# Keys and queries of a head as seven block products, context keys read from memory, turned probabilities evicted by ScalarE

## The chip, the cores and the metric

The kernel runs on one core of a Trainium2 chip. The metric is the device time of one launch in microseconds (us), from the first to the last instruction and what lies around it. The core has five engines that work side by side, each through its own instructions in order: TensorE (PE) multiplies matrices and transposes, VectorE (DVE) and ScalarE (ACT) work element by element and read TensorE's results out of the banks of PSUM, GpSimd (POOL) does the same more slowly, and SyncE (SP) issues transfers between memory and the on-chip buffers.

## What is computed

The reference is one decoder layer on `x` (16 sequences of 256 tokens, width 256) and a context `ctx_1024` (16 × 77 rows, width 256), everything in fp32: three sublayers, each `x = layernorm(x + f(x))`. Cut to what matters:

```python
x = _layernorm(x + _L0_attn_ref(x, ...))              # a small recurrence over time
x = _layernorm(x + _L0_xattn_ref(ctx_1024, x, ...))   # attention, below
x = _layernorm(x + _L0_ffn_ref(x, ...))               # 8 experts, top 2, capacity

# the attention: x = context rows, latents = tokens; H = 8 heads of DH = 128
xn = _layernorm(x, gamma_media, beta_media)
ln = _layernorm(latents, gamma_lat, beta_lat)
q = ln @ Wq + bq
kv_input = jnp.concatenate([xn, ln], axis=1)          # 77 + 256 = 333 rows
k, v = jnp.split(kv_input @ Wkv + bkv, 2, axis=-1)
sim = jnp.einsum('bhid,bhjd->bhij', q * DH ** (-0.5), k)
attn = jax.nn.softmax(sim, axis=-1)
out = jnp.einsum('bhij,bhjd->bhid', attn, v)          # heads are put side by side
return out @ Wo + bo
```

So each of the 16 sequences (called batches below) has 8 heads, and each head has queries for 256 tokens and keys for 333 rows, of which 256 come from the same normalised tokens as the queries and 77 from the context.

## The kernel before

The work goes in three stages. A first stage loads weights, runs the recurrence of batch 0, normalises half of the context rows (five of ten tiles of 128 rows), computes their values for all heads and stores them to memory (`vc_d`), and prepares batch 0. The middle stage walks through all 128 heads (16 batches × 8) in one written-out software pipeline. The last stage runs the experts.

In the middle stage, iteration i does the following in program order. `head_kq(i)`: keys (L587, 333 columns) and queries (L592, 256 columns) of head i, each a sum of two products over the two halves of the width; ScalarE evicts both with the bias (L589, L594). Then the steps that a table lays on this head, such as the recurrence of later batches (`rec_in`, `rec_state`), `prep_keys` (turns the normalised tokens into `kvt`, 333 columns with the context rows copied in by GpSimd, L507), `prep_sums` and `prep_values` (values of the next batch by seven block products, L552), `project_pairs` (the attention's output projection, seven block products of 128×128, L729), `turn_tokens`, `score_experts`, `choose` and `dispatch` (expert choice), and `settle` (stores the batch's tokens, L786). Then `head_out(i−2)`: probabilities times values (L639), evicted by ScalarE (L647). Then `head_softmax(i)`: scores (L602) into one two-bank PSUM tile of which there is only one, the row maximum (DVE, L604), two exponentials with their sums (ScalarE, L608), reciprocal (L610) and normalising (DVE, L613). Then `head_turn(i−1)`: six transposes of the normalised probabilities (L625); DVE evicts four of them (bank pa, L627) and ScalarE two (bank po, L628). The late steps of the table follow.

In the table, batch 0 also computes the values of the other five tiles of context rows (`context`, L470), and each batch prepares its successor. The recurrence of four batches is finished at once (`rec_state`, with a small scan at its end that begins with the product L385). Within these limits a scheduler of the framework chooses the issue order on each engine; where the code says `issue_after`, an instruction is held behind another. SP issues all loads and stores of these stages in one order, among them the values of a batch's context rows (L549), the token stores (L786) and, early on, 34 clears of the expert buffer.

A seven-product scheme forms a 2×2 block matrix product with seven block products instead of eight, from sums and differences of the blocks. The kernel before uses it for the values and for the output projection, the sums of weights being made once.

## Time and profile before

| | |
|---|---|
| median of 3 runs | 1165.93 us (1164.4 to 1166.26) |
| profiled execution | 1174.61 us |
| its span, first to last instruction | 1172.9 us |
| first scores of head (0,0) start | 51.4 us |
| heads | 51.4 to about 1022 us |
| TensorE busy | 1140.7 us (97%), 5436 instructions |
| VectorE busy | 812.1 us (69%) |
| ScalarE busy | 494.5 us (42%) |
| GpSimd busy | 321.2 us (27%) |
| mean granted TensorE clock | 0.998 |

A line of the profile names the source line, the engine, the operation, the tile written and the tiles read, and the shapes. A count follows an x. In timelines the first two numbers are start and duration in microseconds; what stands in brackets is the idle time of the engine before the instruction and who ended it. In groups, total busy time and the mean of one (ns) are followed by the engine's idle time ahead of the group. Where instructions of TensorE overlap, the step from start to start is the price of one, and the duration is longer. Weight loads (PEld) run beside the products.

### The profile page before, as it was taken

The numbers are of one execution on the slowest core, as the hardware profiler recorded it, in microseconds if no ns is written. First come the engines' busy times: TensorE is split into PE (matmuls) and PEld (weight loads), VectorE is DVE, ScalarE is ACT, GpSimd is POOL, SyncE is SP. The second block draws the span as 40 slices with busy tenths as digits, with TensorE's granted clock in tenths as the row PEclk, the third lists the DMA queues.
The fourth block names the chain that finished last, engine by engine and source line by source line (L and its number), as shares of the span: only waits on it lengthen the run. The fifth ranks groups of instructions, "written<-read, shape, count | busy, mean of one in ns | idle before, by whom it ended". The sixth has DMA issues, their size and how long they took to land. (4 is left out here: it accounts for less than half of the span.)

```text
span 1172.9 us, 16419 instructions
## 1 busy us (share of the span) xinstructions
PE 1140.7 (97%) x5436; PEld 833.5 (71%) x5436; DVE 812.1 (69%) x2367; ACT 494.5 (42%) x1298; POOL 321.2 (27%) x564
## 2 busy tenths in 40 slices
PE   7999999999999999999999999999999999999996
PEld 3465676777787877677777777687877778876664
DVE  6655878686757776876678767766576664665665
ACT  3344444443444444444445444444444443523331
POOL 2211243113311331232213322232122212144454
PEclk9999999999999999999999999999999999999999
DMA  7740101001000010000000100000001000045752
GB/s 253 217 144 33 35 22 37 12 28 39 24 25 17 28 37 22 27 29 19 15 10 24 37 14 10 14 19 14 10 14 46 24 10 12 21 162 137 180 161 87
DMA packets 47149, 60.67 MB, mean 52 GB/s; under 512 B 7941, under 2 KB 37102, under 8 KB 47064
## 3 DMA queue, kind: packets, MB, share of 16 engines
q1 hardware_dynamic: 39686, 50.31, 13.5%
q0 software_dynamic: 6048, 9.22, 3.1%
q8 instruction: 43, 0.70, 0.3%
q14 instruction: 42, 0.34, 0.1%
q10 hardware_dynamic: 1330, 0.10, 0.1%
HBM read 36.33 MB, written 30.78 MB: 57 GB/s over the span
## 5 line engine op out<-in xcount | busy, mean ns | idle before, releaser
L639 PE MATMUL po<-ptt,v 128*128 128x256 f32 (+1 forms) x768 | 190.9, 382 | 1.6 <-DVE rs L610 1.6
L639 PEld LDWEIGHTS po<-ptt,v 128*128 128x128 f32 (+1 forms) x768 | 141.5, 190 | 53.1 <-issue 35.5
L587 PE MATMUL pk<-kvt,wkv_s 128*128 128x333 f32 x512 | 165.3, 444 | 0.0
L602 PE MATMUL s<-kt,qt 128*128 128x333 f32 x512 | 164.3, 442 | 0.0
L604 DVE TENSOR_REDUCE nm<-s 128x2 f32<-128x666 f32 x128 | 108.3, 846 | 54.3 <-PE s L602 54.1
L608 ACT ACTIVATE p<-s,nm 128x333 f32<-128x333 f32 x256 | 135.4, 535 | 22.6 <-DVE nm L604 21.9
L647 ACT ACTIVATE ot<-po,bkv_s 128x256 f32<-128x256 f32 x128 | 60.8, 475 | 172.0 <-PE po L639 171.0
L592 PE MATMUL pq<-kvt,wq_s 128*128 128x256 f32 x512 | 131.2, 379 | 0.0
L587 PEld LDWEIGHTS pk<-kvt,wkv_s 128*128 128x128 f32 x512 | 91.1, 191 | 45.9 <-issue 23.2
L602 PEld LDWEIGHTS s<-kt,qt 128*128 128x128 f32 x512 | 96.5, 189 | 30.9 <-issue 0.5
L592 PEld LDWEIGHTS pq<-kvt,wq_s 128*128 128x128 f32 x512 | 96.7, 189 | 30.5 <-issue 0.5
L628 ACT COPY ptt<-pb 77x256 f32<-77x256 f32 x128 | 47.2, 369 | 163.1 <-PE pb L625 163.1
L613 DVE TENSOR_SCALAR pn<-p,rs 128x333 f32<-128x333 f32 x256 | 100.8, 429 | 3.3
L921 POOL DMA_INDIRECT xg<-xs,sidx x64 | 65.6, 1025 | 89.2 <-DVE sidx L918 58.5
L627 DVE COPY ptt<-pa 128x512 f32<-128x512 f32 x128 | 87.2, 682 | 0.6 <-PE pa L625 0.6
L625 PEld LDWEIGHTS pa<-ident,pn 128*128 128x128 f32 x512 | 63.9, 141 | 29.3
L589 ACT ACTIVATE kt<-pk,bkv_s 128x333 f32<-128x333 f32 x128 | 68.9, 538 | 24.6 <-PE pk L587 23.8
L625 PE MATMUL pa<-ident,pn 128*128 128x128 f32 x512 | 76.8, 273 | 0.0
L339 DVE SCALAR_TENSOR_TENSOR cv<-hp,cw,cv 128x512 f32<-128x512 f32 (+1 forms) x108 | 73.9, 691 | 1.4
L594 ACT ACTIVATE qt<-pq,bqs 128x256 f32<-128x256 f32 x128 | 61.0, 477 | 18.8 <-PE pq L592 14.9
L324 PE MATMUL ph<-xT,inw 128*128 128x512 f32 (+1 forms) x144 | 63.4, 570 | 5.0 <-DMA inw<-in_in_wT 4.9
L1183 PE MATMUL pf<-w,it 128*128 128x256 f32 x272 | 61.3, 381 | 2.7 <-ACT ye L1193 1.5
(254 smaller groups left out, 1826.8 us busy)
## 6 DMA issues: line engine op xcount, KB each, us to landing
v<-vc SPq DMA_DIRECT2D x16, 308.0 KB
xg<-zero SPq DMA_DIRECT2D x34, 131.0 KB
xe<-xg SPq DMA_DIRECT2D x8, 524.0 KB
xt<-in_x_in SPq DMA_DIRECT2D x16, 256.0 KB
out<-o SPq DMA_DIRECT2D x16, 256.0 KB
w<-in_w1T SPq DMA_DIRECT2D x8, 512.0 KB
w<-in_w2T SPq DMA_DIRECT2D x8, 512.0 KB
oe<-ye SPq DMA_DIRECT2D x15, 256.0 KB
```

The lines of the kernel that those rows point to most:

```text
L339: V.scalar_tensor_tensor(cv, hp[:, :, k : k + S], cw[:, c, k : k + 1], cv, ALU.mult, ALU.add)
L587: T.matmul(pk[:, 0:J], lhsT=wkv_s[:, k, f], rhs=kvt[:, k, :], start=(k == 0), stop=(k == DC - 1))
L589: A.activation(kt, pk[:, 0:J], AF.Identity, bias=bkv_s[:, h : h + 1])
L592: T.matmul(pq[:, 0:S], lhsT=wq_s[:, k, f], rhs=kvt[:, k, 0:S], start=(k == 0), stop=(k == DC - 1))
L602: T.matmul(s[:, ic, 0:J], lhsT=qt[:, ic * P : (ic + 1) * P], rhs=kt, start=True, stop=True)
L604: V.tensor_reduce(nm, s[:, :, 0:J], AX.X, ALU.max, negate=True)
L608: A.activation(p[:, ic, :], s[:, ic, 0:J], AF.Exp, bias=nm[:, ic : ic + 1], accum_out=sm[:, ic : ic + 1])
L613: V.tensor_scalar(pn[:, ic, :], p[:, ic, :], rs[:, ic : ic + 1], None, ALU.mult)
L625: T.transpose(dst[0:jn, c0 : c0 + P], pn[:, ic, j0 : j0 + jn], ident)
L627: turned = V.tensor_copy(ptt[:, 0:2, :], pt01.rearrange("p (j i) -> p j i", j=2))
L639: T.matmul(po[:, 0:S], lhsT=vs[b][0:jn, jc, h * DH : (h + 1) * DH], rhs=ptt[0:jn, jc, :], start=(jc == 0), stop=(jc == 2),)
L921: dma = G.indirect_dma_start(out=xg[:, :], out_offset=bass.IndirectOffsetOnAxis(ap=sidx[:, t, c : c + 1], axis=0), in_=xs[b][:, t, :], in_ ...
```

## The change

Four things change together.

1. For batches 1 to 15 the tokens' keys and queries of a head are formed as one 2×2 block product (rows: the two halves of the tokens; columns: the head's keys and queries) by seven products of 128×128 instead of eight blocks' worth. The sums of the tokens' blocks are those that the values already use (`tsums`). The sums of weights are made once during batch 0 by DVE (`kq_weights`, which also overwrites a part of the query weights; these are scaled once by ScalarE in `scale_queries`). The products come in two parts: `kq_first` (three products, copied by ScalarE into `u`, one DVE operation) at the start of the iteration before, and `kq_second` (four products, one ScalarE and four DVE operations) after that iteration's output products. So keys and queries are made one head ahead. Batch 0 uses plain products of 256 columns, into one bank. The banks pk and pq now alternate by head.
2. Keys of all context rows are computed once, tile by tile and for all heads (`context_keys`, 16 products of 128 columns a tile; five tiles in the first stage, five during batch 0), evicted with the bias by DVE and stored to memory (`kc_d`, two stores a tile). Each head loads its 77 columns into `kt` (128 partitions of 308 bytes, 39 KB) by SP. The copy of context rows by GpSimd goes away, and `kvt` holds 256 columns.
3. ScalarE evicts the four transposes of bank pa; DVE did that. Probabilities are normalised in place, with three buffers in place of two, and the anchor `turned` is now the last normalising operation.
4. The end of `rec_state` is a step of its own (`rec_scan`), placed behind the output products of the same head. A few buffers share space in other ways.

```diff
--- before
+++ after
@@ -90,6 +90,7 @@
     oe_d = dram.tile([E * CAP + S, D], F32, tag="oe", name="oe")
+    kc_d = dram.tile([P, H, B * M], F32, tag="kc", name="kc")
     vc_d = dram.tile([B * M, INNER], F32, tag="vc", name="vc")
...
@@ -183,9 +184,9 @@
     bl = wpool.tile([P, DC], F32, tag="bl", name="bl")
     emb_s = wpool.tile([P, DC, E], F32, tag="emb", name="emb_s")
     wosum = wpool.tile([P, 3, H // 2, P], F32, tag="wosum", name="wosum")
+    BLOCKS = range(H)
+    kqsum = wpool.tile([P, 3, len(BLOCKS), P], F32, tag="kqsum", name="kqsum")
     wsum = wpool.tile([P, 4, 512], F32, tag="wsum", name="wsum")
-    kvc = wpool.tile([P, DC, B * M], F32, tag="kvc", name="kvc")
     b2 = work.enter_context(tc.tile_pool(name="b2", bufs=2))
     b1 = work.enter_context(tc.tile_pool(name="b1", bufs=1))
...
@@ -284,6 +285,9 @@
     bqs = wpool.tile([P, H], F32, tag="bqs", name="bqs")
     V.tensor_scalar(bqs, bq_s, DH**-0.5, None, ALU.mult)
+    def scale_queries():
+        A.activation(wq_s.rearrange("p k f -> p (k f)"), wq_s.rearrange("p k f -> p (k f)"), AF.Copy, scale=DH**-0.5)
     def load_rest():
         nc.sync.dma_start(wo_s, wo.rearrange("(h p) f -> p h f", p=P))
         nc.sync.dma_start(bo_s, bo.broadcast_to([P, D]))
...
@@ -381,9 +385,18 @@
         dec = aw.tile([P, S], F32, tag="dec", name=f"dec{first}")
         A.activation(dec[R], zb[R], AF.Exp)
         A.activation(dec[R], dec[R], AF.Exp, scale=-1.0)
+        scans[first] = R, rows, members, sg, zb, dec
+        if first == 0:
+            rec_scan(first)
+    scans = {}
+    def rec_scan(first):
+        R, rows, members, sg, zb, dec = scans.pop(first)
         pp = bank(f"pp{first}")
         T.matmul(pp[R, 0:S], lhsT=perm[R, R], rhs=zb[R], start=True, stop=True)
-        bs = aw.tile([P, S], F32, tag="bs", name=f"bs{first}")
+        bs = zb
         A.activation(bs[R], pp[R, 0:S], AF.Tanh, scale=0.5)
         V.scalar_tensor_tensor(bs[R], bs[R], 1.0, pp[R, 0:S], ALU.add, ALU.mult)
         V.tensor_tensor(bs[R], bs[R], sg[R, 0:S], ALU.mult)
...
@@ -442,9 +455,10 @@
             pt = turns[t // 2][:, t % 2, :]
         for k in range(DC):
             T.transpose(pt[:, k * P : k * P + rows], zc[0:rows, 0, k * P : (k + 1) * P], ident[0:rows, 0:rows])
+        kvcs[t] = b2.tile([P, DC, P], F32, tag="kvc", bufs=3, name=f"kvc{t}")
         for k in range(DC):
             A.activation(
-                kvc[:, k, t * P : t * P + rows],
+                kvcs[t][:, k, 0:rows],
                 pt[:, k * P : k * P + rows],
                 AF.Identity,
                 bias=bm[:, k : k + 1],
...
@@ -483,6 +497,34 @@
         if first:
             nc.sync.dma_start(vc_d[t * P : t * P + rows, :], stages[t // 2][0:rows, t % 2, :])
+    def context_keys(t, first):
+        rows = ctx_rows(t)
+        if first:
+            stage = b2.tile([P, 2, 4, P], F32, tag="ot", name=f"kc{t}")
+        for half in range(2):
+            heads = slice(half * 4, half * 4 + 4)
+            if first:
+                kc = stage[:, half]
+                pk = bank(f"pkc{t}_{half}", ("pk", "pq", "pa", "po")[(2 * t + half) % 4], 1)
+            else:
+                kc = b1.tile([P, 4, P], F32, tag=("xb", "x2")[half], name=f"kc{t}_{half}")
+                pk = bank(f"pkc{t}_{half}")
+            pk = pk.rearrange("p (h r) -> p h r", h=4)
+            for h in range(4):
+                f = half * 512 + h * DH
+                for k in range(DC):
+                    T.matmul(
+                        pk[:, h, 0:rows],
+                        lhsT=wkv_s[:, k, f : f + DH],
+                        rhs=kvcs[t][:, k, 0:rows],
+                        start=(k == 0),
+                        stop=(k == DC - 1),
+                    )
+            bias = bkv_s[:, heads].unsqueeze(2).broadcast_to([P, 4, rows])
+            V.tensor_tensor(kc[:, :, 0:rows], pk[:, :, 0:rows], bias, ALU.add)
+            nc.sync.dma_start(kc_d[:, heads, t * P : t * P + rows], kc[:, :, 0:rows])
     stages, kvt_ends = {}, {}
     turned = None
...
@@ -503,8 +545,7 @@
     def prep_keys(b):
         zl = zs.pop(b)
-        kvt = b2.tile([P, DC, J], F32, tag="kvt", name=f"kvt{b}")
-        G.tensor_copy(kvt[:, :, S:J], kvc[:, :, b * M : (b + 1) * M])
+        kvt = b2.tile([P, DC, S], F32, tag="kvt", name=f"kvt{b}")
         pt = bank(f"pt{b}")
         for k in range(DC):
             d = slice(k * P, (k + 1) * P)
...
@@ -578,21 +619,71 @@
     kts, qts, pns, ptts, tsums = {}, {}, {}, {}, {}
-    def head_kq(b, h):
+    def kq_weights(h):
+        f = slice(h * DH, (h + 1) * DH)
+        t = lambda i: kqsum[:, i, h - BLOCKS[0], :]
+        V.tensor_tensor(t(0), wq_s[:, 0, f], wkv_s[:, 0, f], ALU.subtract)
+        V.tensor_tensor(wq_s[:, 0, f], wq_s[:, 1, f], wq_s[:, 0, f], ALU.subtract)
+        V.tensor_tensor(t(1), wq_s[:, 1, f], t(0), ALU.subtract)
+        V.tensor_tensor(t(2), wkv_s[:, 1, f], t(1), ALU.subtract)
+    pks, parts_kq = {}, {}
+    def kq_product(b, h, which, first):
+        f = slice(h * DH, (h + 1) * DH)
+        t = lambda i: kqsum[:, i, h - BLOCKS[0], :]
+        w = (wkv_s[:, 0, f], wkv_s[:, 1, f], wq_s[:, 1, f], t(2), t(0), t(1), wq_s[:, 0, f])
+        for r, n in which:
+            T.matmul(
+                pks[b, h][:, r * P : (r + 1) * P],
+                lhsT=w[n - 1],
+                rhs=tsums[b][n - 1],
+                start=first and r == 0,
+                stop=True,
+                skip_group_check=True,
+            )
+    def kq_first(b, h):
+        f = slice(h * DH, (h + 1) * DH)
         kvt = kvts[b]
-        f = slice(h * DH, (h + 1) * DH)
-        pk = bank(f"pk{b}_{h}", "pk", 1)
-        for k in range(DC):
-            T.matmul(pk[:, 0:J], lhsT=wkv_s[:, k, f], rhs=kvt[:, k, :], start=(k == 0), stop=(k == DC - 1))
-        kt = b2.tile([P, J], F32, tag="kt", name=f"kt{b}_{h}")
-        A.activation(kt, pk[:, 0:J], AF.Identity, bias=bkv_s[:, h : h + 1])
-        pq = bank(f"pq{b}_{h}", "pq", 1)
-        for k in range(DC):
-            T.matmul(pq[:, 0:S], lhsT=wq_s[:, k, f], rhs=kvt[:, k, 0:S], start=(k == 0), stop=(k == DC - 1))
-        qt = b2.tile([P, S], F32, tag="qt", name=f"qt{b}_{h}")
-        A.activation(qt, pq[:, 0:S], AF.Identity, bias=bqs[:, h : h + 1], scale=DH**-0.5)
-        kts[b, h], qts[b, h] = kt, qt
+        kts[b, h] = kt = b2.tile([P, J], F32, tag="kt", name=f"kt{b}_{h}")
+        qts[b, h] = qt = b2.tile([P, S], F32, tag="qt", name=f"qt{b}_{h}")
+        pks[b, h] = pk = bank(f"pk{b}_{h}", ("pk", "pq")[h % 2], 1)
+        nc.sync.dma_start(kt[:, S:J], kc_d[:, h, b * M : (b + 1) * M])
+        if b == 0 or h not in BLOCKS:
+            for k in range(DC):
+                T.matmul(pk[:, 0:S], lhsT=wkv_s[:, k, f], rhs=kvt[:, k, :], start=(k == 0), stop=(k == DC - 1))
+            A.activation(kt[:, 0:S], pk[:, 0:S], AF.Identity, bias=bkv_s[:, h : h + 1])
+            for k in range(DC):
+                T.matmul(pk[:, S:], lhsT=wq_s[:, k, f], rhs=kvt[:, k, :], start=(k == 0), stop=(k == DC - 1))
+            A.activation(qt, pk[:, S:], AF.Identity, bias=bqs[:, h : h + 1])
+            return
+        kq_product(b, h, ((0, 1), (1, 5), (2, 7)), True)
+        parts_kq[b, h] = u = b2.tile([P, 3, P], F32, tag="ukq", bufs=1, name=f"ukq{b}_{h}")
+        A.copy(u.rearrange("p r d -> p (r d)"), pk[:, 0 : 3 * P])
+        V.scalar_tensor_tensor(u[:, 1, :], u[:, 1, :], bqs[:, h : h + 1], u[:, 2, :], ALU.add, ALU.add)
+    def kq_second(b, h):
+        pk = pks.pop((b, h))
+        if (b, h) not in parts_kq:
+            return
+        pks[b, h] = pk
+        kq_product(b, h, ((3, 6), (0, 2), (2, 4), (1, 3)), False)
+        del pks[b, h]
+        u, kt, qt = parts_kq.pop((b, h)), kts[b, h], qts[b, h]
+        A.activation(kt[:, 0:P], pk[:, 0:P], AF.Identity, bias=bkv_s[:, h : h + 1])
+        u0 = u[:, 0, :]
+        V.tensor_tensor(u0, u0, pk[:, 3 * P :], ALU.add)
+        V.scalar_tensor_tensor(kt[:, P:S], pk[:, 2 * P : 3 * P], bkv_s[:, h : h + 1], u0, ALU.add, ALU.add)
+        V.scalar_tensor_tensor(qt[:, 0:P], pk[:, P : 2 * P], bqs[:, h : h + 1], u0, ALU.add, ALU.add)
+        V.tensor_tensor(qt[:, P:S], u0, u[:, 1, :], ALU.add)
     def head_softmax(b, h):
...
@@ -602,16 +693,16 @@
             T.matmul(s[:, ic, 0:J], lhsT=qt[:, ic * P : (ic + 1) * P], rhs=kt, start=True, stop=True)
         nm = small.tile([P, 2], F32, tag="nm", name=f"nm{b}_{h}")
         V.tensor_reduce(nm, s[:, :, 0:J], AX.X, ALU.max, negate=True)
-        p = b2.tile([P, 2, J], F32, tag="p", name=f"p{b}_{h}")
+        p = b2.tile([P, 2, J], F32, tag="p", bufs=3, name=f"p{b}_{h}")
         sm = small.tile([P, 2], F32, tag="sm", name=f"sm{b}_{h}")
         for ic in range(2):
             A.activation(p[:, ic, :], s[:, ic, 0:J], AF.Exp, bias=nm[:, ic : ic + 1], accum_out=sm[:, ic : ic + 1])
         rs = small.tile([P, 2], F32, tag="rs", name=f"rs{b}_{h}")
         V.reciprocal(rs, sm)
-        pn = b2.tile([P, 2, J], F32, tag="pn", name=f"pn{b}_{h}")
         for ic in range(2):
-            V.tensor_scalar(pn[:, ic, :], p[:, ic, :], rs[:, ic : ic + 1], None, ALU.mult)
-        pns[b, h] = pn
+            ends = V.tensor_scalar(p[:, ic, :], p[:, ic, :], rs[:, ic : ic + 1], None, ALU.mult)
+        pns[b, h] = p
+        return ends
     def head_turn(b, h):
...
@@ -624,10 +715,9 @@
                 dst = pt01 if jc < 2 else pt2
                 T.transpose(dst[0:jn, c0 : c0 + P], pn[:, ic, j0 : j0 + jn], ident)
         ptt = b2.tile([P, 3, S], F32, tag="ptt", name=f"ptt{b}_{h}")
-        turned = V.tensor_copy(ptt[:, 0:2, :], pt01.rearrange("p (j i) -> p j i", j=2))
+        A.copy(ptt[:, 0:2, :], pt01.rearrange("p (j i) -> p j i", j=2))
         A.copy(ptt[0:M, 2, :], pt2[0:M, 0:S])
         ptts[b, h] = ptt
-        return turned
     def head_out(b, h):
...
@@ -965,8 +1061,10 @@
+                amid(b, 0, rec_scan, nb)
+                amid(b, 0, rec_scan, nb)
...
@@ -982,6 +1080,7 @@
+            amid(0, 2, rec_scan, 1)
...
@@ -992,6 +1091,7 @@
+                amid(0, h + 1, context_keys, FIRST_CTX + h, False)
...
@@ -1001,6 +1101,9 @@
+    for h in BLOCKS:
+        behind(0, min(h, H - 2), kq_weights, h)
...
@@ -1020,23 +1123,29 @@
     context_turn(0, True)
     context_turn(1, True)
     context(0, True)
+    context_keys(0, True)
     rec_state(0, 0)
     context(1, True)
+    context_keys(1, True)
     context_turn(2, True)
     context_turn(3, True)
     rec_add(0, 1)
     context(2, True)
+    context_keys(2, True)
     rec_out(0)
     prep_norm(0)
     context(3, True)
+    context_keys(3, True)
     context_turn(4, True)
     prep_keys(0)
     context(4, True)
+    context_keys(4, True)
     wparts = weight_sums()
     prep_sums(0)
     for n in range(3):
         for second in (False, True):
             prep_values(0, n, second)
+    scale_queries()
     load_rest()
...
@@ -1260,22 +1369,30 @@
     heads = [(b, h) for b in range(B) for h in range(H)]
+    kq_first(*heads[0])
+    kq_second(*heads[0])
     for i in range(len(heads) + 2):
         if i == len(heads) - 2 * H:
             rec.close()
             open_early()
         if i == len(heads) - 2:
             rows[0] = Rows(0)
+        if i + 1 < len(heads):
+            kq_first(*heads[i + 1])
         if i < len(heads):
-            head_kq(*heads[i])
             for f, args in steps[heads[i]]:
                 f(*args)
         if i >= 2:
             head_out(*heads[i - 2])
         if i < len(heads):
-            head_softmax(*heads[i])
+            for f, args in mid_steps[heads[i]]:
+                f(*args)
+        if i + 1 < len(heads):
+            kq_second(*heads[i + 1])
+        if i < len(heads):
+            turned = head_softmax(*heads[i])
         if 1 <= i <= len(heads):
-            turned = head_turn(*heads[i - 1])
+            head_turn(*heads[i - 1])
         if i < len(heads):
             for f, args in late_steps[heads[i]]:
                 f(*args)
```

## The prediction

> **What bounds the kernel now.** I read first the busy shares of the engines, then the slices of the span, then TensorE's timeline in a plain stretch, then the windows from one head's scores to the next, and last the waits.
>
> ```profile
> PE 1140.7 (97%) x5436; PEld 833.5 (71%) x5436; DVE 812.1 (69%) x2367; ACT 494.5 (42%) x1298; POOL 321.2 (27%) x564
> PE   7999999999999999999999999999999999999996
> DVE  6655878686757776876678767766576664665665
> PEclk9999999999999999999999999999999999999999
> ```
> TensorE (PE) is busy in 9 tenths or more of all slices but the first and last, at full clock. It is the bound; but VectorE (DVE) reaches 8 tenths in places. A piece of TensorE's timeline gives the pace of each shape, as start to next start (the durations overlap):
> ```profile
> 576.03 1.28 PE L587 MATMUL pk<-kvt,wkv_s 128*128 128x333 f32 x4
> 577.15 1.02 PE L592 MATMUL pq<-kvt,wq_s 128*128 128x256 f32 x4
> 578.01 1.05 PE L729 MATMUL pw<-wo_s,ot 128*128 128x128 f32 x8
> 578.90 1.06 PE L729 MATMUL pw<-wosum,osum 128*128 128x128 f32 x8
> ...
> 580.69 1.46 PE L639 MATMUL po<-ptt,v 128*128 128x256 f32 x6
> 581.99 1.28 PE L602 MATMUL s<-kt,qt 128*128 128x333 f32 x4
> ```
> Keys take 1.12 us (577.15 − 576.03; 0.280 an instruction), queries 0.86 (0.215), eight 128-column instructions 0.89 (0.112). One product in fp32 is two instructions. Nothing stands idle between them.
> The next rows are windows from the start of one head's scores to the next, for heads 0, 1 and 3 of batch 9 (columns: length, then busy PE, PEld, DVE, ACT, POOL):
> ```profile
> 626.40:632.70 6.30, 6.30 (x34) 4.60 (x33) 6.19 (x12) 3.31 (x9) 1.12 (x1) 1.00 0.00 1
> 632.70:640.40 7.70, 7.70 (x49) 6.69 (x48) 7.08 (x18) 3.27 (x9) 4.54 (x11) 1.00 0.26 75
> ...
> 649.50:656.30 6.80, 6.80 (x30) 4.79 (x29) 6.55 (x21) 3.27 (x9) 5.23 (x13) 1.00 0.00 0
> ```
> In these heads DVE is within 0.1 to 0.6 us of TensorE. Whole batches (8 to 11, the same view) leave it more room:
> ```profile
> 566.60:626.40 59.80, 59.80 (x292) 45.02 (x291) 39.55 (x107) 27.60 (x73) 10.63 (x18) 1.00 0.04 12
> 626.40:684.80 58.40, 58.40 (x299) 44.88 (x298) 46.76 (x130) 26.12 (x71) 20.34 (x39) 1.00 0.10 30
> 684.80:751.00 66.20, 64.90 (x338) 47.22 (x338) 46.42 (x117) 29.93 (x78) 13.73 (x21) 1.00 0.04 11
> 751.00:807.80 56.80, 56.80 (x296) 44.31 (x295) 42.77 (x124) 24.67 (x69) 17.66 (x36) 1.00 0.06 18
> ```
> In the waits, the max of the scores (DVE) stands 48 times idle for TensorE; in the other 80 heads DVE comes to it late; and SP's queue waits for others.
> ```profile
> DVE nm L604 <- PE s L602: 54.1, 48, 2.0
> SPq L549 <- PE po L639: 384.3, 13, 40.6
> SPq L786 <- POOL o L785: 379.0, 16, 46.4
> ```
>
> The costs of evictions are from the groups by shape (count, total busy, mean ns):
> ```profile
> L627 DVE COPY ptt<-pa 128x512 f32<-128x512 f32 x128 | 87.2, 682 | 0.6 <-PE pa L625 0.6
> ...
> L743 DVE TENSOR_TENSOR xb<-xb,u 128x128 f32<-128x128 f32 x28 | 8.1, 290 | 5.4 <-ACT u L741 5.0
> ```
> ```profile
> L741 ACT COPY u<-pw 128x384 f32<-128x384 f32 x14 | 6.7, 480 | 28.3 <-PE pw L729 28.3
> ```
>
> **The change part by part.** All sums are against the profiled execution, 1174.61 us, which is 8.68 above the median 1165.93.
>
> *Keys and queries by blocks.* Removed: per head, 4 instructions of 0.280 and 4 of 0.215, 1.984 us. Added: 7 products, 14 instructions of 0.112, 1.568. That is −0.416 a head on a gapless engine; 120 heads (batches 1 to 15): −49.9. Batch 0 keeps plain products, but its keys fall from 333 to 256 columns: 4 × 0.065 = −0.26 a head, −2.1.
> TensorE could be charged otherwise for narrow products. [...] The rows above scale with the width (0.112, 0.215, 0.280), and the measured rows decide.
>
> *Context keys once.* Added: for each of nine full tiles 16 products, 32 × 0.112 = 3.58 us; the tenth has 80 rows, between 2.2 (by width) and 3.58 (no gain): 2.9. Five tiles, 17.9, fall before the heads, where TensorE is the bound with 4.9 us of gaps in 51; I let the new work fill 1.5: +16.4 (ends 13 and 17.9). Five, 17.2, fall into batch 0, which has no gaps: +17.2 − 2.1 = +15.1. Their 20 evictions are DVE operations like the 128x512 copy from PSUM, about 0.69 each.
>
> *DVE.* Per head of batches 1 to 15 it loses the 128x512 copy of L627 (0.682, at pace 0.60). It gains four operations on 128x128 (0.29 each by L743 and L746, with dependent starts 0.21 to 0.33) and one scalar_tensor_tensor of the same size, about 1.31 in all. Net +0.71 a head, +5.7 a batch. In batch 0 come 32 operations for the weight sums (32 × 0.26 = 8.3) and 10 evictions (6.9), less 8 × 0.60; DVE goes from 54.6 of 82.6 to about 65 of 98: hidden.
>
> *ScalarE.* Per head it loses the evictions kt (0.538) and qt (0.477) and gains u (128x384, 0.480 by L741), half a kt (about 0.35) and the 128x512 eviction (0.585 by L480): +0.4, 3.3 to about 3.75 in a plain head of 4.63. That fits, but in order: the next head's second block products wait for u, the outputs for both turned copies, the next scores for the exponentials, since the score bank is single. Scaling the query weights (2.2 by four 128x512 copies) is early and hidden.
>
> *Loads of kt.* 128 loads of 39 KB, each an issue of 0.31 us on SP by the v load, 40 us on a queue that stands waiting 763 us in the two rows above. A load is issued when the scores two heads back have read the buffer and is wanted one to two heads later, 6 to 13 us. On the last chain a 524 KB transfer took 3.73 us; that is the upper end, so the load is hidden by at least 2 us. They stand behind v loads and the out stores; an out store that POOL delays holds all behind it. In the new issue order the out store of batch 5 stands just before the load for head 5 of batch 6; the trace has that store at 475.3 and those scores at 485.2, 9.9 us, of which 6 stay after the transfer. I take zero; one late store costs what POOL is late. The 20 key stores and the clears (0.49 us each from 43 to 70) share SP in batch 0; the first two kt loads stand ahead of the clears.
> [...]
>
> *The recurrence's scan* goes behind the output products: the three waits near 265.6, 506.8 and 747.9 (1.34 to 1.47 each) can close: −4.4 at most, 0 at least if DVE is later; −2.5. The POOL copy of context rows goes; POOL bounds nothing.
>
> *Stalls that replace the bound.* TensorE's head shrinks by 0.42 and DVE's grows by 0.71. Over whole batches (−3.3 and +5.7 to the four rows above) DVE stays below: 45 to 53 of 53 to 63 us, 80 to 95%. Head by head it does not: in batch 9, head 0 goes to 5.9 PE against 6.9 DVE, head 1 to 7.3 against 7.8, head 3 to 6.4 against 7.3. Adding these excesses over a period of four batches (about ten heads) gives 8 us if no head can lend to the next, 0 if all can. Following the issue order of batches 8 to 10 by hand with these durations, I find TensorE waiting for expert counts whose inputs come late from DVE (about 0.6 and 1.05), for output sums behind a max reduction (1.05), for turned copies (0.2 to 0.65): about 2 us in each heavy stretch and 0.2 in light heads, 5.6 in four batches. Over 15 batches with batch 1 and 15 at 2 each: +22 (ends 0 and 28 by the excesses; 50 if every head lasts as long as before). Batch 0: exponentials behind the late first tiles, +3 (0 to 6).
>
> Sum: 16.4 + 15.1 + 3 − 49.9 + 22 − 2.5 = +4.1, so 1178.7 profiled, 1170 in the median. Without any stall it is −20.9, 1145; every microsecond of stall adds one.
>
> **Rivals.**
> - *TensorE remains the bound* (stalls up to 15 us): the other side, 1145 to 1160, likeliest 1153, faster. For it: DVE has 5 to 20% left in each batch, and the products stand a head ahead, so that lateness of one head can be taken back in the next light one. Against: the score bank is single and DVE's lag in heads 0 to 3 has no light head between. It decides from 18.6 us of stalls downwards.
> - *DVE becomes the bound of most heads* (stalls 35 to 60): 1180 to 1205, likeliest 1195, where a head lasts as before and the 49.9 are lost. For it: max, exponentials, normalise, four block operations and the next max form a loop through two engines that both work in order. Against: batches 12, 14 and 15 have DVE at 60% of TensorE.
> - *kt loads come late*: one wait of 3 us per batch behind an out store would be +45, about 1215. Against: the 6 us left above.
> The change does do what it says; a head without block products exists only in batch 0.
>
> **How the numbers follow.** The forecast's case (stalls 15 to 35, 1160 to 1180) 0.46; TensorE remains the bound 0.28; DVE the bound 0.20; late loads 0.06. Measurement tells 0.2%, 2.3 us: faster is below 1163.6, slower above 1168.3. Of the forecast's 0.46 I place 0.06 below, 0.14 within and 0.26 above. Faster 0.34, same 0.14, slower 0.52. The range leaves out 0.05 of the first rival's low end, 0.06 of late loads and about 0.06 of the DVE case's high end: 1150 to 1193. The likeliest case alone: 1160 to 1180.
>
> **What would show it.** Right: block products 8 in about 0.9 us; the first scores start near 68 (51.4 before); batch 0 near 98 to 101; TensorE at about 94 to 95% with idle time of 20 to 30 us between 150 and 1040, its releasers DVE (osum, on, the last evictions of kt and qt) and the turned copies on ScalarE; DVE near 910 us busy; no wait of scores on a DMA. Wrong: TensorE still without gaps in batches 2 to 15 (first rival), gaps in nearly all heads with DVE at 95% (second), or scores waiting for kt from a DMA (third); or 128-column products slower than 0.112 where the weights change with each.

## The result

The changed kernel takes 1171.24 us in the median (1169.41 to 1174.10), the kernel before 1165.16 (1164.18 to 1166.48) on the same chip: a ratio of 1.0053, 95% interval 1.0043 to 1.0063. It is 0.5% slower. The forecast was 1170 and slower.

The profiled execution of the changed kernel took 1172.73 us (span 1171.0), near its own median, while that of the kernel before lay 8.7 above the median of its first three runs. So the two profiles differ by −1.9 us and the medians by +6.1, and the comparison has to be made stage by stage. The page of the changed kernel, busy shares and slices:

```profile
PE 1138.1 (97%) x6476; PEld 881.2 (75%) x6476; DVE 889.6 (76%) x2891; ACT 539.4 (46%) x1427; POOL 316.4 (27%) x548
PE   7999999999999999999999899999999999999996
DVE  6754579979886878798868887988678766756765
PEclk9999999999999989999999999999999999999999
```

TensorE is as busy as before by this view, with a thousand instructions more. The one fallen digit in PEclk, and DVE's slices of 8 and 9, are where to look. The stages, as windows of the trace. Of the kernel before: batch 0, then batches 1 to 15, then the rest:

```profile
51.40:134.00 82.60, 82.07 (x317) 48.98 (x316) 54.63 (x116) 38.94 (x99) 10.65 (x25) 1.00 0.27 83
```
```profile
134.00:1022.60 888.60, 880.86 (x4474) 671.39 (x4473) 631.17 (x1735) 396.21 (x1074) 224.69 (x402) 1.00 0.07 22
1022.60:1172.90 150.30, 135.47 (x527) 92.09 (x525) 93.35 (x418) 44.18 (x94) 70.95 (x76) 0.98 0.50 142
```

Of the changed kernel, batch 0 and then batches 4, 5, 8 and 9 (the first column after the limits is the length, then busy PE, PEld, DVE, ACT, POOL, clock, DMA):

```profile
69.40:167.80 98.40, 97.05 (x489) 67.15 (x489) 58.24 (x131) 42.13 (x106) 9.98 (x24) 1.00 0.27 83
350.40:407.00 56.60, 56.60 (x341) 45.51 (x340) 44.54 (x138) 29.74 (x81) 10.84 (x17) 1.00 0.09 25
407.00:469.40 62.40, 59.55 (x344) 47.15 (x343) 51.41 (x162) 29.20 (x80) 19.39 (x38) 0.95 0.13 37
586.80:643.40 56.60, 56.60 (x341) 45.53 (x340) 44.55 (x138) 29.73 (x81) 10.80 (x17) 1.00 0.06 18
643.40:704.10 60.70, 56.59 (x344) 44.79 (x343) 51.65 (x162) 29.11 (x80) 19.57 (x38) 1.00 0.12 34
```

and its batches 1 to 15 and the rest:

```profile
167.80:1025.60 857.80, 845.43 (x5178) 681.10 (x5177) 694.87 (x2217) 433.84 (x1191) 222.25 (x389) 1.00 0.10 29
1025.60:1171.00 145.40, 133.63 (x524) 91.60 (x522) 91.83 (x409) 45.24 (x95) 71.20 (x76) 0.98 0.51 147
```

| stage | before | changed | difference | forecast |
|---|---|---|---|---|
| to the first scores | 51.4 | 69.4 | +18.0 | +16.4 |
| batch 0 | 82.6 | 98.4 | +15.8 | +18.1 |
| batches 1 to 15 | 888.6 | 857.8 | −30.8 | −30.4 |
| the rest (experts) | 150.3 | 145.4 | −4.9 | 0 |

Batches 4 and 8 take 3.2 us less than before (59.8), all that part 1 of the forecast can give (8 × 0.416 = 3.3). Batches 5 and 9 took 58.4 before and got longer: they lose the whole gain and 4.0 or 2.3 more. The other batches from 2 on take 2.0 to 3.2 less. What ended TensorE's idle time, in the changed kernel's waits (total, times, longest):

```profile
PE pa L716 <- DVE p L703: 3.6, 2, 1.8
PE s L693 <- ACT p L699: 2.9, 8, 1.3
PE pw L819 <- DVE ot L795: 2.5, 3, 1.1
```

The two waits of the transposes for the normalised probabilities (L703) are at the starts of batches 5 and 9. TensorE there (start, duration, and in brackets the idle time and who ended it):

```profile
406.97 1.28 PE L693 MATMUL s<-kt,qt 128*128 128x333 f32 x4
410.05 0.33 PE L716 MATMUL pa<-ident,p 128*128 128x128 f32 x1 [1.80 <-DVE p L703]
```

DVE in the same stretch, and then POOL beside it:

```profile
405.55 0.35 DVE L670 SCALAR_TENSOR_TENSOR ukq<-ukq,bqs 128x128 f32<-128x128 f32 x1
405.83 2.28 DVE L341 TENSOR_SCALAR cv<-hp,cw,cb 128x512 f32<-128x512 f32 x1
408.15 0.75 DVE L343 SCALAR_TENSOR_TENSOR cv<-hp,cw,cv 128x512 f32<-128x512 f32 x1
408.82 0.16 DVE L701 RECIPROCAL rs<-sm 128x2 f32<-128x2 f32 x1
408.94 0.75 DVE L343 SCALAR_TENSOR_TENSOR cv<-hp,cw,cv 128x512 f32<-128x512 f32 x1
409.61 0.69 DVE L703 TENSOR_SCALAR p<-p,rs 128x333 f32<-128x333 f32 x2
```
```profile
404.96 1.52 POOL L1011 DMA_INDIRECT xg<-xs,sidx  x1 [0.30 <-issue]
406.49 1.30 POOL L350 TENSOR_TENSOR sums<-hs 128x512 f32<-128x512 f32 x1
```

DVE has no gap here: it is working off a chunk of the recurrence's convolution (L341, L343) between the steps of the softmax. The first of these takes 2.28 us where its median is 0.55, and ends at 408.11, 0.32 us after POOL's addition beside it (406.49 to 407.79). The normalising that TensorE waits for comes at 409.61.

### The profile page after: what moved, and what is told of

Read it like the earlier page. It is cut to its first block, busy times and chain, and to the rows that moved or that the text cites. A ratio compares the mean times of both kernels' runs of the same rounds, so it can differ in the third digit from the quotient of the medians.

```text
span 1171.0 us, 19506 instructions
## 1 busy us (share of the span) xinstructions
PE 1138.1 (97%) x6476; PEld 881.2 (75%) x6476; DVE 889.6 (76%) x2891; ACT 539.4 (46%) x1427; POOL 316.4 (27%) x548
## 5 line engine op out<-in xcount | busy, mean ns | idle before, releaser
L718 ACT COPY ptt<-pa 128x512 f32<-128x512 f32 x128 | 74.8, 584 | 150.5 <-PE pa L716 150.5
L737 ACT ACTIVATE ot<-po,bkv_s 128x256 f32<-128x256 f32 x128 | 60.7, 474 | 99.7 <-PE po L729 99.1
L703 DVE TENSOR_SCALAR p<-p,rs 128x333 f32<-128x333 f32 x256 | 95.8, 415 | 2.9
L640 PE MATMUL pk<-tsum,kqsum 128*128 128x128 f32 x480 | 94.5, 278 | 2.0 <-ACT ukq L669 1.8
L640 PE MATMUL pk<-tsum,wq_s 128*128 128x128 f32 x480 | 93.2, 276 | 0.0
L640 PE MATMUL pk<-kvt,wkv_s 128*128 128x128 f32 x480 | 93.0, 276 | 0.0
L640 PEld LDWEIGHTS pk<-tsum,kqsum 128*128 128x128 f32 x480 | 80.5, 191 | 14.9 <-ACT ukq L669 7.3
L716 PEld LDWEIGHTS pa<-ident,p 128*128 128x128 f32 x512 | 63.6, 141 | 34.2 <-DVE p L703 5.9
L716 PE MATMUL pa<-ident,p 128*128 128x128 f32 x512 | 77.8, 274 | 3.6 <-DVE p L703 3.6
L343 DVE SCALAR_TENSOR_TENSOR cv<-hp,cw,cv 128x512 f32<-128x512 f32 (+1 forms) x108 | 73.6, 689 | 1.4
L640 PEld LDWEIGHTS pk<-tsum,wq_s 128*128 128x128 f32 x480 | 73.3, 193 | 0.0
L669 ACT COPY ukq<-pk 128x384 f32<-128x384 f32 x120 | 57.5, 479 | 27.3 <-DVE qt L686 24.3
L328 PE MATMUL ph<-xT,inw 128*128 128x512 f32 (+1 forms) x144 | 63.7, 571 | 5.7 <-DMA inw<-in_in_wT 5.0
```

Source lines behind the costliest of these rows:

```text
L328: T.matmul(ph, lhsT=inw[:, k, c * P : (c + 1) * P], rhs=xTs[pr][:, k, cols], start=(k == 0), stop=(k == DC - 1),)
L343: V.scalar_tensor_tensor(cv, hp[:, :, k : k + S], cw[:, c, k : k + 1], cv, ALU.mult, ALU.add)
L640: T.matmul(pks[b, h][:, r * P : (r + 1) * P], lhsT=w[n - 1], rhs=tsums[b][n - 1], start=first and r == 0, stop=True, skip_group_check=True,)
L703: ends = V.tensor_scalar(p[:, ic, :], p[:, ic, :], rs[:, ic : ic + 1], None, ALU.mult)
L716: T.transpose(dst[0:jn, c0 : c0 + P], pn[:, ic, j0 : j0 + jn], ident)
L718: A.copy(ptt[:, 0:2, :], pt01.rearrange("p (j i) -> p j i", j=2))
```

## The experiments

The theory after the comparison: what the block products lose is DVE's lateness, two thirds of it at the starts of batches 5 and 9, with POOL's hold on a DVE operation as the last straw. The rivals: ScalarE's order, with a fifth eviction a head on it, holds TensorE; or working one head ahead costs something by itself. These runs fell on four chips. On one of them the kernel before takes 1165 us, as in the first comparison, on the three others 1174 to 1175. Each ratio is to runs of the kernel before on the same chip, and kernels of different chips are compared by their stages.

| kernel | median (before, same chip) | ratio, interval | batches 1–15 | of it TensorE busy |
|---|---|---|---|---|
| before, profiled again (one run) | 1174.72 (1173.62) | | 888.4 | 880.7 |
| changed, again | 1170.86 (1165.41) | 1.0044, 1.0031–1.0057 | 856.0 | 842.5 |
| plain products | 1212.24 (1173.62) | 1.0312, 1.0281–1.0343 | 889.0 | 871.9 |
| plain, wide | 1169.55 (1165.41) | 1.0030, 1.0018–1.0041 | 853.7 | 851.5 |
| DVE evicts | 1205.01 (1173.62) | 1.0250, 1.0220–1.0279 | 884.5 | 850.8 |
| chunk moved | 1174.57 (1173.62) | 1.0008, 0.9994–1.0023 | 857.7 | 846.4 |
| no sums on POOL | 1170.61 (1165.41) | 1.0045, 1.0032–1.0057 | 854.2 | 845.9 |
| plain in 22 heads | 1166.46 (1165.41) | 0.9999, 0.9989–1.0009 | 849.8 | 843.9 |
| plain in 16 heads | 1173.04 (1175.20) | 0.9983, 0.9974–0.9992 | 854.7 | 844.7 |
| joined operations | 1178.28 (1174.41) | 1.0040, 1.0027–1.0053 | 860.9 | 842.2 |
| … sums in pieces | 1179.76 (1174.41) | 1.0056, 1.0044–1.0068 | 860.9 | 841.8 |
| … and plain in 12 heads | 1172.83 (1174.41) | 0.9992, 0.9981–1.0004 | 854.1 | 840.4 |

**Both kernels again.** No edit. Expected:

> The kernel before, unchanged, profiled a second time. Its first profile ran 1174.6 us, 8.7 above the median of its timed runs; the changed kernel's profile ran 1172.7, only 1.5 above its own. If the first profile was disturbed in the expert tail (150.3 us there, 145.4 in the changed kernel), the second should have the first scores near 51.4, batch 0 near 82.6, batches 1 to 15 near 888.6 as before, and a tail of 141 to 146, some 1164 to 1170 in all. If the whole kernel varies, the middle stage should differ by several microseconds.

> The changed kernel, unchanged, on the same chip as the three kernels below, since the kernel before took 1165 us on one chip and 1174 on another. Expected: the stages of its first profile (first scores at 69.4, batch 0 98.4, batches 1 to 15 857.8 us) within 1 us each but the first, and 0.0% to 0.6% above the kernel before.

The kernel before: first scores at 53.3, batch 0 82.6, batches 1 to 15 888.4 (888.6 in the first profile), the rest 148.7. The middle stage repeats to 0.2 us, but the tail did not shorten as I had expected. This profile fell on a chip where the whole takes 1174. Its stages fit a first profile taken on such a chip, which is not on record, and say nothing of the tail on the chip where the whole takes 1165.

The changed kernel: 69.1, 98.4, 856.0, 145.4. The 1.8 us less in the middle are batch 5 alone (60.7 in place of 62.5), which is told in the last section.

**Part 1 undone: plain products in all heads.** The edit:

```diff
-        if b == 0 or h not in BLOCKS:
+        if True:
...
-    for h in BLOCKS:
-        behind(0, min(h, H - 2), kq_weights, h)
```

> Part 1 undone alone: keys and queries of all heads by plain products of 256 columns, evicted by ScalarE, still one head ahead, with context keys from memory and the turned probabilities on ScalarE. TensorE per head of batches 1 to 15: 8 x 0.216 against 14 x 0.112, +0.16, +19.2 in 120 heads; DVE loses 1.3 us a head. Theory (what was lost in batches 1 to 15, about 19 us of the 50 saved, is lateness of DVE): the lost 19 come back, so 1171 give or take 5, with no idle TensorE at heads (5,0) and (9,0). Rival (ScalarE's fixed order, with the turned probabilities now on it, holds TensorE): its work grows slightly, the loss stays, 1190.

Batches 1 to 15 take 889.0 us, 31 more than in the changed kernel, and neither theory gave that. The waits of TensorE and its weight loads tell why:

```profile
PE pk L664 <- ACT kt L662: 7.6, 13, 1.9
```
```profile
PEld pk L664 <- ACT kt L662: 34.7, 83, 2.3
```

The query products write the bank that holds the keys, and are made to wait until ScalarE has evicted these. The edit had added a wait. So the test was made again with both products ahead of both evictions:

```diff
             for k in range(DC):
                 T.matmul(pk[:, 0:S], ...)
-            A.activation(kt[:, 0:S], ...)
             for k in range(DC):
                 T.matmul(pk[:, S:], ...)
+            A.activation(kt[:, 0:S], ...)
             A.activation(qt, pk[:, S:], ...)
```

> Part 1 undone more cleanly: plain products of 256 columns for all heads, but keys and queries both multiplied before either is evicted. In the first form the query products stood 7.6 us in all behind the eviction of the keys, which share their bank, and their weight loads 34.7. TensorE's work is 19.2 us above the changed kernel's, DVE's 157 us (120 x 1.31) below. Theory (DVE lateness costs the changed kernel about 19 us in batches 1 to 15): these come back, so 0 to +6 us against the changed kernel. Rival (order on ScalarE, or work one head ahead by itself, costs as much): +19 to +30, as in the first form.

The whole takes 1169.55 against 1170.86 (0 to 6 more was expected), the middle 853.7 against 856.0. The window of its batches 1 to 15:

```profile
169.10:1022.80 853.70, 851.48 (x4471) 672.36 (x4471) 564.04 (x1624) 438.18 (x1192) 222.18 (x389) 1.00 0.10 29
```

TensorE stands idle for 2.2 us in 854, where the changed kernel had 13.6 in its second profile; DVE has 131 us less to do and ScalarE 4 more. So a fifth eviction on ScalarE and work one head ahead cost nothing by themselves, and both rivals fall. The edit takes away more than DVE's work, though: with it go ScalarE's copy `u` and the second part of the products that waits for it. TensorE waited for that copy 2.5 us in all in the second profile of the changed kernel (1.8, and its weight loads 7.3, in the first), and no run takes it away alone. Summing TensorE's steps from start to start by line, the block products take 192.2 us where plain ones take 205.9, so they save 13.7 (19.2 if none were late). The output products take 6.5 more, the scores 5.5, the values 2.2, the transposes 0.9, and nothing is left. In this kernel the seven products are worth nothing. What batches 1 to 15 gain comes from the context keys: 77 columns fewer in every head's key products are worth 31 us (120 × 4 × 0.065, an estimate from the paces of 333 and 256 columns), and the kernel with plain products has them too. They cost 18.0 and 15.8 us ahead of that, so that they no more than pay for themselves.

**Part 3 undone: DVE evicts again.**

```diff
-        A.copy(ptt[:, 0:2, :], pt01...)
+        V.tensor_copy(ptt[:, 0:2, :], pt01...)
```

> Part 3 undone alone: DVE, not ScalarE, evicts the four transposes (0.60 at pace). Theory (DVE is late in its busiest stretches): more stretches of DVE above TensorE; it gains 4.8 us a batch and has 2 to 10 left of 54 to 63: +10 to +30, 1181 to 1201. Rival (ScalarE's order): ScalarE loses 0.58 a head, and turned probabilities are out sooner: 1160 to 1168.

Batches 1 to 15 take 884.5, 27 more than in the first profile of the changed kernel, within the theory's 10 to 30, and the rival's sign is wrong. The middle of this kernel, and its first waits of TensorE:

```profile
167.80:1052.30 884.50, 850.75 (x5170) 683.74 (x5169) 753.86 (x2326) 380.32 (x1070) 219.65 (x389) 0.99 0.10 28
```
```profile
PE pk L640 <- ACT ukq L669: 10.4, 15, 1.5
PE po L729 <- DVE ptt L718: 6.2, 15, 1.0
```

DVE has 59 us more to do. Against the second profile of the changed kernel (856.0, at full clock) the middle is 28.5 longer: 20 of it are idle TensorE (33.7 against 13.6) and 8 longer instructions. Up to 5.1 of these 8 can be the clock, which was granted at 0.50 in three stretches of 3.4 us each (0.95 in the mean of batch 5; half of 10.2, an estimate). The copy L669 that TensorE waits for is itself held by DVE: in both kernels it waits some 24 us, in about 20 places, for DVE's last block operation (L686), as `u` has one buffer. A second buffer was not tried. Without part 3, batches 1 to 15 would have kept 4 us of their gain (884.5 against 888.6 before).

**A chunk of the convolution moved** from head 0 to head 2 of batches 5 and 9:

```diff
-  ((0, 5), (0, 7), (1, 0), (1, 5))
+  ((0, 5), (0, 7), (1, 2), (1, 5))
```

> The changed kernel with one chunk of the recurrence's input work (convolution of 512 channels x tokens: four DVE operations of 0.55 to 0.75, the gate, a sum on POOL) moved from head 0 to head 2 of batches 5 and 9. Theory (DVE, filled there by two such chunks and the block operations, and held once by POOL, is late at (5,0) and (9,0)): batches 5 and 9 lose 7.3 and 5.5 us against the block products' saving; most of it, 9 to 13, comes back: 1159 to 1162. Rival (ScalarE's order): no DVE work is taken away, and ScalarE's chunk only moves with it: 1168 to 1172.

Batches 5 and 9 go to 58.1 each, 4.4 and 2.6 less than in the first profile and 2.6 each less than in the second. But batches 2, 6 and 10 take 0.7 to 0.8 more, 3, 7 and 11 1.0 to 1.1 and 4 and 8 0.5: 857.7 in all, where the changed kernel took 857.8 and 856.0. The expected 9 to 13 us did not come. The scheduler ordered the recurrence's scan anew: TensorE now waits for the scan's result (L405, 2.2 us in all, in three places) and before its product (L398, 1.4 in all, in three), neither of which it did in the changed kernel.

**No sums on POOL.**

```diff
-            sums[pr] = aw.tile([P, PT], F32, tag="sums", ...)
...
-        if c > 0 and pr > 0:
-            G.tensor_tensor(sums[pr], hs[:, 0, :] if c == 1 else sums[pr], hs[:, c, :], ALU.add)
```

> POOL no longer adds the recurrence's four chunks (128x512, 1.28 us each); TensorE sums them instead by three more small products for each member, about 0.7 us in each of three batches. At (5,0) and (9,0) a DVE operation of 0.55 us took 2.28 and 2.27, until such an addition on POOL ended, and one of 0.28 took 1.12. Theory (POOL's addition holds DVE, and that is the last straw there): both are back at 0.55 and 0.28, the idle 1.96 and 1.95 us of TensorE behind them shrink below 0.5, and the half clock after the first is gone: batches 5 and 9 together 4 to 7 us shorter, the whole 2 to 5. Rival (DVE's own work is too much there anyway): the durations fall, but TensorE waits as long; +1 to +2.

DVE at the start of batch 5, POOL beside it, and the windows of batches 4, 5 and 6:

```profile
406.37 0.34 DVE L667 SCALAR_TENSOR_TENSOR ukq<-ukq,bqs 128x128 f32<-128x128 f32 x1
406.64 0.55 DVE L340 TENSOR_SCALAR cv<-hp,cw,cb 128x512 f32<-128x512 f32 x1
```
```profile
405.79 1.53 POOL L1008 DMA_INDIRECT xg<-xs,sidx  x1 [0.30 <-issue]
```
```profile
351.20:407.80 56.60, 56.60 (x341) 45.54 (x340) 44.50 (x139) 29.73 (x81) 10.46 (x17) 1.00 0.09 25
407.80:465.90 58.10, 56.44 (x344) 44.77 (x343) 48.60 (x161) 29.20 (x80) 16.11 (x34) 1.00 0.13 39
465.90:530.20 64.30, 63.99 (x415) 49.31 (x415) 51.87 (x154) 32.96 (x87) 11.23 (x21) 1.00 0.10 29
```

The operation is back at 0.55, TensorE's wait for the normalising (L703 in the changed kernel) is gone, and batches 5 and 9 take 58.2, 2.5 less each. So POOL's hold was shown to be the last straw, worth 5 us of the 11 that these two batches lost in the second profile. It is the addition that holds, for here the operation ran its 0.55 us inside the other work that POOL had beside it (L1008). The whole moved by −0.25, inside the noise, because TensorE's extra products cost 1.3 in each of batches 0, 6 and 10 and 0.7 in batch 2, where I had worked out 0.7 in three.

**Plain products in some heads.** First in 22 heads (6 and 7 of batches 4, 8, 12; 0 to 3 of 1, 5, 9, 13); then in 16, with the original query weights of those heads kept. In the first trial these heads multiplied by weights that the block sums had overwritten, so their queries are other numbers; operations and shapes are the same.

```diff
-        if b == 0 or h not in BLOCKS:
+        if b == 0 or (b % 4 == 0 and h > 5) or (b % 4 == 1 and h < 4):
```

> The changed kernel with plain products (both before either eviction) in 22 heads only: heads 6 and 7 of batches 4, 8, 12 and heads 0 to 3 of batches 1, 5, 9, 13; also that order in batch 0. TensorE +0.16 in each, +3.5; DVE -1.31 in each. Theory (DVE is late from head 6 of batches 4 and 8 on): batches 5 and 9 lose 7.3 and 5.5 against the block products' saving, of which 9 to 12 come back: 5 to 9 us below the changed kernel, so below the kernel before. Rival: no lateness is removed: +3 to +5.

Its windows of batches 4 and 5:

```profile
352.40:409.40 57.00, 57.00 (x317) 45.37 (x317) 41.66 (x125) 29.96 (x81) 10.21 (x17) 1.00 0.09 27
409.40:466.20 56.80, 56.29 (x332) 44.91 (x331) 46.56 (x145) 29.02 (x79) 19.04 (x38) 1.00 0.13 38
```

Batches 5 and 9 go from 60.7 to 56.8, the 9 to 12 us expected of both became 7.8; the middle from 856.0 to 849.8. The whole is 4.4 us below the changed kernel (5 to 9 expected) and level with the kernel before.

> The changed kernel with plain products for keys and queries (both multiplied before either is evicted) in 16 heads: 6 and 7 of batches 4 and 8, 0 to 3 of batches 1, 5 and 9, with the original query weights of those heads kept beside the block sums, where the first trial of such heads had taken weights that the sums had overwritten. Theory (two thirds of what the block products lose is lost where DVE is late from (4,6) and (8,6) on): batches 1 to 15 in 848 to 851 us (856 to 858 in the changed kernel), batches 5 and 9 at 56.8 each; 5 to 8 us below the changed kernel, 1163 to 1167 where the kernel before takes 1165, and below it by 0.3 to 0.6% where that takes 1174, as the tail there is longer for the kernel before. Rival (the issue order, which the scheduler makes anew for each edit, decides more than DVE's load, as in the kernel with the joined DVE operations): anywhere from 850 to 862 in batches 1 to 15.

Batches 5 and 9 are at 56.8 again, 854.7 in all where 848 to 851 was expected: 3, 7 and 11 took 1.1 more, and 2, 6 and 10 0.8 more, by the same waits at the scan that the moved chunk had brought. It is below the kernel before by 0.17% (0.08 to 0.26) on a chip where that takes 1175, and 0.3 to 0.6% was expected there. On the chip where that takes 1165 this kernel was not run.

**Less DVE work for the same result.** All keys of a head take the queries' bias, which falls out of the softmax; two operations become one:

```diff
-        V.scalar_tensor_tensor(u[:, 1, :], u[:, 1, :], bqs[:, h : h + 1], u[:, 2, :], ALU.add, ALU.add)
+        V.tensor_tensor(u[:, 1, :], u[:, 1, :], u[:, 2, :], ALU.add)
...
-        V.tensor_tensor(u0, u0, pk[:, 3 * P :], ALU.add)
-        V.scalar_tensor_tensor(kt[:, P:S], pk[:, 2 * P : 3 * P], bkv_s[:, h : h + 1], u0, ALU.add, ALU.add)
-        V.scalar_tensor_tensor(qt[:, 0:P], pk[:, P : 2 * P], bqs[:, h : h + 1], u0, ALU.add, ALU.add)
+        V.scalar_tensor_tensor(u0, pk[:, 3 * P :], bqs[:, h : h + 1], u0, ALU.add, ALU.add)
+        V.tensor_tensor(two, pk[:, P : 3 * P]..., u0 for both, ALU.add)
```

> The changed kernel with less DVE work for the same result: a constant added to all keys of a head adds the same to all scores of a query and falls out of the softmax, so all keys take the queries' bias in place of their own. Then the shared block sum carries the bias, one scalar_tensor_tensor early becomes a plain addition, and the two operations that finish half the keys and half the queries (0.346 and 0.341 us) become one of 256 columns. That is about 0.3 us of DVE less in each of 120 heads, 36 in all, TensorE's work unchanged; batch 0 multiplies before it evicts. Theory (DVE lateness): 3 to 8 us below the changed kernel. Rival (DVE's total is not what holds TensorE, only POOL's hold on it at (5,0) and (9,0) is): 0 to 1 below.

DVE has 21 us less to do in the middle (673.6 against 694.7), and the middle takes 860.9, 4.9 more than in the second profile of the changed kernel. That contradicts a theory of DVE's total. Batches 5 and 9 are 0.6 and 0.7 shorter; what is lost lies in batches 3, 7 and 11 (1.0 each) and 2, 6 and 10 (0.4 to 0.8), with waits at the scan as when the chunk was moved (2.6 and 2.1 us in all), and in batch 13 (1.9). TensorE and DVE at batch 5, head 1:

```profile
415.90 1.06 PE L826 MATMUL pw<-wosum,osum 128*128 128x128 f32 x8
419.10 1.29 PE L826 MATMUL pw<-wo_s,ot 128*128 128x128 f32 x8 [2.15 <-DVE ot L802]
```
```profile
416.02 1.47 DVE L151 TENSOR_SCALAR xs<-xt,mva,ra 128x256 f32<-128x256 f32 x2 [0.51 <-POOL ra L137]
417.41 0.28 DVE L693 TENSOR_TENSOR kq<-ukq 128x128 f32<-128x128 f32 x1
417.61 0.84 DVE L702 TENSOR_REDUCE nm<-s 128x2 f32<-128x666 f32 x1
418.37 0.67 DVE L802 TENSOR_TENSOR ot<-ot 128x512 f32<-128x512 f32 x1
```

The wait at the start of batch 5 is gone, but the projection now waits 2.15 us for an operation that stands on DVE behind a normalisation of tokens, which itself waits for POOL, and behind the maximum. In the changed kernel the same wait was 1.1. After it TensorE ran 3.4 us at a granted clock of 0.50 (0.97 in the mean of the batch), and so it did in batch 9, which is worth up to 3.4 us of the 4.9 (half of 6.8, an estimate). It is a matter of which short operation stands behind which long one, and with DVE this full (673.6 of 860.9 us) the new orders of this kernel and of the one with the moved chunk each had such places.

> The last kernel, and POOL adds the recurrence's chunks in four pieces of 128 columns rather than one of 512 (1.28 us). Theory (a DVE operation is held until the POOL addition beside it ends): no DVE operation is held longer than about 0.4 us, and (5,0) and (9,0) come 1 to 2.5 us shorter each: 2 to 5 below the last kernel. Rival (the hold lasts as long as POOL works on the tile, pieces or not): 0.

The longest of the operations so held falls from 1.32 to 0.82 us (that one beside another addition of POOL's, of 128x256), so pieces do limit the hold. The middle stays at 860.9 (batch 9 1.3 shorter, batch 7 2.4 longer, as the half clock now fell in batch 7 in place of batch 9); the 2 to 5 us did not come.

> The last kernel, and plain products for keys and queries in twelve heads (6 and 7 of batches 4 and 8, 0 to 3 of batches 5 and 9), whose original query weights are kept beside the block sums. TensorE +0.16 in each, +1.9; DVE about -1.0 in each. Theory: batches 5 and 9 reach 56.8 each as in the first trial of such heads (60.7 in the changed kernel), and the whole is 6 to 11 us below the changed kernel, 1160 to 1165 where that runs 1171, at or below the kernel before. Rival (little lateness is left to remove there): +1 to +2 over the last kernel.

854.1, batches 5 and 9 at 56.5: 6.8 below the last kernel, against the rival, and 0.9992 of the kernel before. Against the changed kernel the middle is 1.9 shorter, where 6 to 11 for the whole was expected; on this chip that kernel was not run.

What the runs support in the end: the loss is lateness of DVE. That is shown for POOL's hold on it (5 us), and by adding work to DVE (eviction). Taking its work away where it is late (plain products, in all heads or some) agrees, but takes the copy `u` along. The loss is not proportional to DVE's total. The order that the scheduler makes around the projection and the scan is worth 1 to 5 us either way, in part by way of the clock. What remains open is the tail of the kernel before: on the chip of the first comparison the stages above leave about 3 of the 6.1 us unexplained, and by subtraction they lie outside batches 0 to 15. No profile of that kernel on that chip exists. The loss seems to depend on the chip: the kernel with the moved chunk, whose middle is that of the changed kernel, stands at 1.0008 of the kernel before (0.9994 to 1.0023) where that takes 1174.

## Why the prediction was right

**Keys and queries by blocks, −49.9.** Right in the price: the products cost 0.112 us an instruction in every form, and batches 4 and 8 show the whole −3.2. That narrow products could be charged otherwise, a doubt of the prediction, was not borne out: in the changed kernel 128 columns took 0.112 us, 256 0.216 and 333 0.280. The term holds two things that should have stood apart: about 31 for the narrower keys, which are the context keys' gain, and 19 for the seven products, which lateness ate whole.

**Context keys, +16.4 and +17.2 − 2.1.** Measured +18.0 and +15.8 with what stalled. I had let the new products fill 1.5 us of idle TensorE before the heads; it fell from 9.1 (51.4 − 42.3 busy) to 7.4 (69.3 − 61.9), as assumed, though the 4.9 of gaps that I named was the first wait for a DMA alone. But from 10 to 20 us the mean granted clock was 0.83, where the first profile of the kernel before had 1.00; that is worth about 1.7 us (10 × 0.17, an estimate), and it makes up the difference: against the second profile of the kernel before, with a clock of 0.97 up to its first scores (53.3 × 0.03 = 1.6, by the same estimate), the step is 69.4 − 53.3 = 16.1. The last section comes back to it. In batch 0 I gave stalls 3 us; 0.7 is what is left.

**DVE, +0.71 a head.** Measured in batches 1 to 15: 694.9 − 631.2 = 63.7 us, 0.53 a head. Two runs tell the parts: plain products free 131 us of DVE, 1.09 a head where I had 1.31, and the eviction put back costs it 59, 0.49 a head where I had 0.60. Normalising in place took 415 ns where it took 429.

**Stalls, +22, less 2.5 for the scan.** The sum held: 857.8 and 856.0 are 19.1 and 17.3 above 888.6 − 49.9 = 838.7, where the forecast says 19.5. Its parts did not. I spread it as about 2 us over each heavy stretch and 0.2 over each light head, with waits for expert counts among them. No wait for counts appeared, most batches lost 0.1 to 1.3, and two batches lost 12.8 of the 19.1 (7.3 and 5.5). The three waits ahead of the scan's product, 1.3 us each before, are gone whole, 3.9 where I took 2.5. The wait that carries it (transposes for normalised probabilities, 1.8 us, with DVE held by POOL) was not on my list, though the trace of before had such holds (1.44 us for a normalising of 0.39). That step was right in size by luck. The wait of the projection behind a maximum, which I had put at 1.05, was there (1.1).

**Loads of kt, 0.** Right: a median of 1.7 us from issue to landing, and no score waited for a DMA. SP's queue stood 118 us for POOL's stores in all, and no score waited for it.

**The median.** I took 8.68 us off for what lies between a profiled execution and the median. The changed kernel's own offset is 1.5. By stages the change is +3.0 before the tail, the medians differ by 6.1, and the forecast +4.1 lies between. Taking off 8.68 was an error of its own: the second profile of the kernel before lay 1.1 above the median of its chip, so that the 8.68 looks like a difference between chips and not one between profiled runs and others. So the closeness of 1170 to 1171 is better than its working, and in part luck.

**What I said would show it.** First scores at 69.4 (68 forecast), batch 0 98.4 (98 to 101), idle TensorE in the middle of 12.4 (20 to 30 forecast), its busy share 97% and not 94 to 95. A stall shows mostly as longer instructions here: idle time grew by 4.6 us (from 7.7), while busy time lies 14.5 above the 880.9 − 49.9 that the saving would leave. DVE at 890, not 910.

**The rivals.** TensorE as the bound: its deciding point, 18.6 us of stalls, was missed by little, for in the same terms batches 1 to 15 had 21.6 (−30.8 + 49.9 + 2.5). But with plain products in 22 heads they had 13.6, which by my sum, with 1.4 in batch 0, makes 1160 and some 6 us less than the kernel before, and the kernel is level with it. So the point lay too high by what the sum lacks outside batches 1 to 15. DVE as the bound of most heads: it needs more DVE work than this change brings, as the eviction put back on DVE shows (884.5, near the 888.6 at which all is lost).

## What to carry to other kernels

A gain in products on the busiest engine has to be paid in additions on another: before taking it, look at the second engine head by head, not by its share of the span, and price what it delivers late. With TensorE busy for 97% here and DVE for 76%, the moved chunk and the joined operations each made a new order with new waits (2.2 us in all in three places, 2.15 in one), so that gains of that size had to be read from stages and not from the sum of instruction times. And where one change brings several savings, each should be taken out alone: here the context keys cost 34 us and bring back about 31, and the seven products, which the kernel also carries, bring nothing.
